# A two-layer CIN kernel: all chunk pairs of the second layer in Strassen's form, four equal stages, half of each T2 on VectorE

## The chip, the cores and the metric

The kernel runs on one core of a Trainium2 chip. The metric is device microseconds from launch to end; each time given is a median of several executions. The profile is one execution taken by the hardware profiler; its span runs from the first instruction to the last. In it PE is TensorE (PEld its weight loads), DVE is VectorE, ACT is ScalarE, POOL is GpSimd and SP the engine that issues most transfers.

## The reference, cut to what matters

```python
ROWS, FIELDS, EMB = 4096, 32, 16

def _cin_layer(out, x, W, b, gamma, beta):
    r, _, e = x.shape
    h = jnp.einsum('rne,rfe->rnfe', out, x).reshape(r, -1, e)    # all products of two fields
    h = jnp.einsum('rce,oc->roe', h, W) + b[None, :, None]       # 128 outputs
    return _batchnorm(h, gamma, beta)                            # mean and variance over rows and e

h1 = _cin_layer(x, x, W1, b1, g1, beta1)                         # 32*32 products
out, direct1 = (h1[:, :64], h1[:, 64:])
direct2 = _cin_layer(out, x, W2, b2, g2, beta2)                  # 64*32 products
return jnp.concatenate([direct1, direct2], axis=1).sum(axis=-1)
```

A site is one (row, e); there are 65,536. Each layer multiplies fields of a site with each other, contracts the products with a weight matrix to 128 outputs, and normalizes. All is fp32.

## The kernel before

The first layer (up to about 490 us of the span) works on 128 tiles of 512 sites and is not touched. The second layer works on `NC = 64` pairs of tiles; index `c` is the pair. The contraction over 2048 products is cut into 16 chunks of 128: four stages (`STAGES = (3, 0, 1, 2)`, index `k` in the order run, `i` the value), and in each stage two chunk pairs `q = 0, 1`. For one chunk pair the work is a product of 2 x 2 blocks: the weights give blocks a11, a21, a12, a22 (64 outputs of the 128, one of the two chunks), the field products give b11, b12, b21, b22 (one of the two tiles, one of the two chunks). The ordinary form needs 8 matmul calls of 128 x 64 weights against 128 x 512 products. Strassen's form (in Winograd's variant) needs seven, X1 to X7, with sums of weights (`s_sb`, made once) and sums of products:

- T3 = b22 - b12 comes out of the multiplication itself, since `bx` holds differences of inputs;
- T2 = b11 + T3, T1 = b22 - T2, T4 = b21 - T2 are made by vector engines.

In a stage, ScalarE makes two factors (`factor`, L646: the first layer's kept output, normalized, into PSUM), VectorE makes two groups of products of 128 x 2048 (`multiply`, L636): `z[:, 0::3]` (b11, b21) from the first and `z[:, 1:3]` (T3, b22) from the second. GpSimd then makes T (`sum_products`, L672): T2 in one instruction of 1024 columns, T1 and T4 in one of 2048. Stage 3 in `i` (`PLAIN`, the first run) has its q = 0 in the ordinary form and only q = 1 in Strassen's; there (`sum_half`, L681) VectorE makes its single T2, reading a copy of b11 that ScalarE has put into PSUM, and GpSimd makes T1 and T4 in 1024 columns. For c = 0 the last stage is wholly ordinary.

Each matmul writes the lower or upper 64 partitions of a PSUM bank, and the calls alternate between the halves, so that two run beside each other. `Sums` (L655) holds four banks of the six in the pool: x11 (X1 in two parts, one for each half), x62, x34, x57. The matmuls X5 and X4 of a stage (`x54`) are queued behind X3 and X2 of the next, except in the last stage, where they come at once.

When the four stages of a pair are done, `combine` (L734) adds the banks into the four output blocks: two ScalarE evictions and an add for X1 (`both`, L741), then `e[:, 0]` (L747), `u2` on ScalarE, `u3` (L754), a copy of half of `u3` on ScalarE, two more adds (L759, L760), squares for the variance on ScalarE, and a reduction over 16 on VectorE (L779). It is a generator: its steps are taken between the instructions of the next pair's stages, by calls of `step()` at fixed places. `idle` holds small VectorE tasks (statistics of the first layer, differences of inputs) of which one is taken in a pair.

The order on each engine is written out by hand: `queue(engine, ...)` (L226) ties each instruction behind the one queued before on that engine. The pools limit how far an engine runs ahead: three buffers of z, two of t, two of PSUM for factors and the copy of b11 together (`factors`), one of each tile of `combine`.

Every VectorE add of the second layer is recorded at L634, every ScalarE copy and factor at L631, every matmul at L670; they are told apart by tile names (`th`, `both`, `u`, `e`, `f`, `b`).

Of the kernel before, what the change touches and what calls it, by code (L numbers as in the profile page):

```python
# [56 lines left out]
PLAIN = 3  # L58
STAGES = (3, 0, 1, 2)

MINUS = ((PLAIN, 0), (2, 0), (2, 1))
# [7 lines left out]
def tile_cin(ctx: ExitStack, tc: tile.TileContext, xa, xb, xr, w1, w1m, w2, bn, out):  # L69
# [191 lines left out]
    with ExitStack() as one:  # L261
# [31 lines left out]
        neg_sb = const.tile([P, len(MINUS), 2, KEEP], FP, tag="neg", name="neg_sb")  # L293
# [3 lines left out]
        def combine_weights():  # L297

            w = w2_sb.rearrange("p (i j) o -> p i j o", j=4)
            a11, a21, a12, a22 = (w[:, :, j : j + 2, m] for j in (0, 2) for m in (low, high))  # L300
            s1, s2, s3, s4 = (s_sb[:, k] for k in range(4))
            minus = []
            for k, (i, q) in enumerate(MINUS):
                minus.append((neg_sb[:, k, 0], a21[:, i, q], a11[:, i, q], ALU.subtract))
                nc.vector.tensor_scalar(neg_sb[:, k, 1], a21[:, i, q], -1.0, None, ALU.mult)
# [236 lines left out]
    hpool = ctx.enter_context(tc.tile_pool(name="hpool", bufs=1))  # L542
# [58 lines left out]
    nc.vector.tensor_copy(b2_swapped[low], b2[high])  # L601
# [53 lines left out]
    class Sums:  # L655


        def __init__(self):

            banks = [psum.tile([P, T], FP, tag="ps", name=name) for name in ("x11", "x62", "x34", "x57")]  # L660
            x11, x62, x34, x57 = self.banks = banks
            self.of = {
                6: x62[low], 2: x62[high], 3: x34[low], 4: x34[high], 5: x57[low], 7: x57[high], 1: x11[low], 0: x11[high]
            }
            self.started = set()
# [6 lines left out]
    def sum_products(z):  # L672

        t = tpool.tile([P, 3, 2, T], FP, tag="t", name="t")
        queue("pool", lambda: nc.gpsimd.tensor_tensor(t[:, 0], z[:, 1], z[:, 0], ALU.add))  # L675

        twice = t[:, 0].unsqueeze(1).to_broadcast([P, 2, 2, T])
        queue("pool", lambda: nc.gpsimd.tensor_tensor(t[:, 1:3], z[:, 2:4], twice, ALU.subtract))  # L678
        return t

    def sum_half(z, b11):  # L681

        t = hpool.tile([P, 3, 1, T], FP, tag="th", name="th")
        add(t[:, 0, 0], z[:, 1, 1], b11)
        twice = t[:, 0].to_broadcast([P, 2, T])
        queue("pool", lambda: nc.gpsimd.tensor_tensor(t[:, 1:3, 0], z[:, 2:4, 1], twice, ALU.subtract))  # L686
        return t

    class Stage:


        def __init__(self, sums_, i, z, t, plain, last):

            self.matmul, self.last, self.i = sums_.matmul, last, i
            self.w = [weights(i, q) for q in range(2)]
            self.b11, self.t3, self.b22, self.b21 = ([z[:, k, q] for q in range(2)] for k in range(4))
            self.qs = tuple(q for q in range(2) if q not in plain)

            self.t2, self.t1, self.t4 = ({q: t[:, k, q - self.qs[0]] for q in self.qs} for k in range(3))

        def two(self, low_first, *halves):
            for x, w, b, stop in halves if low_first else halves[::-1]:
                self.matmul(x, w, b, stop and x in self.last)

        def ordinary(self, low_first, q):
            a11, a21, a12, a22, s1, s2, s3, s4 = self.w[q]
            minus_s3, minus_a21 = (neg_sb[:, MINUS.index((self.i, q)), k] for k in range(2))
            for x, u, y, v in ((3, s4, 2, a11), (5, s1, 4, a21)):
                self.two(low_first, (x, u, self.b22[q], False), (y, v, self.b11[q], False))
            for x, u, y, v in ((3, minus_s3, 2, a12), (5, minus_a21, 4, a22)):  # L710
                self.two(low_first, (x, u, self.t3[q], q == 1), (y, v, self.b21[q], q == 1))

        def x1(self, low_first):

            halves = [(x, self.w[q][0], self.b11[q], True) for x, q in zip((1, 0), self.qs)]
            if len(self.qs) == 1 and not low_first:
                halves[0] = (0, *halves[0][1:])
            self.two(low_first, *halves)

        def products(self, low_first, x, kx, bx, y, ky, by):  # L720
            for q in self.qs:
                stop = q == 1
                self.two(low_first, (x, self.w[q][kx], bx[q], stop), (y, self.w[q][ky], by[q], stop))

        def x32(self, low_first):
            self.products(low_first, 3, 7, self.b22, 2, 2, self.b21)

        def x67(self, low_first):
            self.products(low_first, 6, 5, self.t2, 7, 6, self.t3)

        def x54(self, low_first):
            self.products(low_first, 5, 4, self.t1, 4, 3, self.t4)

    def combine(c, sums_):  # L734

        x11, x62, x34, x57 = sums_.banks
        both = cpool.tile([P, T], FP, tag="both", name="both")
        act(both[low], x11[high])
        act(both[high], x11[low], bias=b2[low])
        yield  # L740
        add(both, both, x11)  # L741
        yield

        e = cpool.tile([P, 2, T], FP, tag="e", name="e")
        if idle:
            dve(idle.pop(0))
        add(e[:, 0], both, x62)  # L747
        yield
        u2 = cpool.tile([P, T], FP, tag="u2", name="u2")
        act(u2[low], e[low, 0], bias=b2[low])  # L750
        act(u2[high], e[low, 0], bias=b2_swapped[low])
# [25 lines left out]
        yield  # L777
        dve(
# [4 lines left out]
        if c < MOST:  # L783
            queue("act", lambda: add_square(c, 1, e))
# [10 lines left out]
    steps = iter(())  # L795

    def step(count=1):
        for _ in range(count):
            next(steps, None)

    for c in range(NC):
        raw, b, bx = loaded(c)
# [14 lines left out]
        f1 = factor(raw[STAGES[0]], STAGES[0], 0)  # L817
        for k, i in enumerate(STAGES):

            z = z2pool.tile([P, 4, 2, T], FP, tag="zz", name="zz")  # L820
            if c == k == 0:

                f2 = factor(raw[i], i, 1)
                for q in range(2):
                    multiply_part(z[:, 0::3], f1, b, q)
                    multiply_part(z[:, 1:3], f2, bx, q)
                b11 = factors.tile([P, T], FP, tag="f", name="b11")
                act(b11, z[:, 0, 1])
            else:
                multiply(z[:, 0::3], f1, b)  # L830

            if k > 0:
                step()
            if c > 0 or k > 0:
                f2 = factor(raw[i], i, 1)
                if k == 2:

                    step()
                if i == PLAIN:
                    b11 = factors.tile([P, T], FP, tag="f", name="b11")  # L840
                    act(b11, z[:, 0, 1])
                multiply(z[:, 1:3], f2, bx)

            plain = (0,) if i == PLAIN else (0, 1) if c == 0 and k == 3 else ()
            if i == PLAIN:
                t = sum_half(z, b11)
            elif not plain:
                t = sum_products(z)
            if k in (1, 2):

                step()
            if k < 3:
                f1 = factor(raw[STAGES[k + 1]], STAGES[k + 1], 0)
            if k < 3:

                step()
# [3 lines left out]
            low_first = c % 2 == 0  # L860
            rest = not low_first
            last = range(8) if k == 3 else ()
            if c == 0 and k > 1:
                last = ((0, 1, 6, 7), (2, 3, 4, 5))[k - 2]
            stage = Stage(sums_, i, z, t, plain, last)
            if i == PLAIN:
                stage.ordinary(low_first, 0)
            if len(plain) == 2:
                stage.ordinary(rest, 0)
            else:  # L870
                stage.x1(low_first if i == PLAIN else rest)
                stage.x32(rest)
            if k > 0:
                waiting.x54(rest)
            if len(plain) == 2:
                stage.ordinary(rest, 1)
            else:
                stage.x67(rest)
                if k == 3:
                    stage.x54(rest)  # L880
            waiting = stage
# [8 lines left out]
        steps = combine(c, sums_)  # L890

    assert not sums_left
    step(8)
# [27 lines left out]
    with tc.issue_after(lasts["dve"].ins):  # L921
        step()
# [58 lines left out]
```

## Time and profile before

| | |
|---|---|
| time, median of 3 | 2084.3 us (2084.09 to 2085.0) |
| span of the profiled execution | 2082.0 us |
| granted TensorE clock, mean | 0.997 |
| VectorE, products of 128 x 2048 in layer two | 510 instructions, 583.3 + 582.4 us |
| GpSimd, T1 and T4 of 2048 columns | 191 instructions, 871.4 us, 4562 ns each |
| GpSimd, T2 of 1024 columns | 191 instructions, 453.1 us, 2372 ns each |
| VectorE, T2 of one half (`th`) | 64 instructions, 44.1 us, 689 ns each |
| VectorE waiting for PE before products of layer two | 54.3 us in 119 waits |

The chain of waits follows the work back from the last instruction to what released each step. A row of the timeline gives start and duration in us, engine, line, operation, output and input names, shapes, and in brackets the idle time before it and what ended it. Durations of neighbours can overlap a little, so the cost of an instruction in a full queue is read from the starts.

### The profile page before, as it was taken

How to read it: one execution, taken by the hardware profiler on the slowest of the kernel's cores; microseconds unless marked ns; L12 is line 12 of the kernel's file. 1: busy time of each engine (PE TensorE's matmuls, PEld its weight loads, DVE VectorE, ACT ScalarE, POOL GpSimd, SP SyncE). 2: the span in 40 equal slices, each digit the busy share in tenths (PEclk: the TensorE clock that was granted, in tenths of full speed). 3: DMA queues.
4: the chain of work that ended last, by engine and by line, in shares of the span. 5: the costliest groups of instructions: out<-in, count | busy, mean ns of one | idle time of the engine just before them, and what ended most of it. 6: DMA issues, size and time to landing. Idle time of an engine off the chain costs nothing.

```text
span 2082.0 us, 23630 instructions
## 1 busy us (share of the span) xinstructions
PE 2061.8 (99%) x8634; PEld 927.9 (45%) x8634; DVE 1901.4 (91%) x1391; ACT 998.9 (48%) x1594; POOL 1471.8 (71%) x453
## 2 busy tenths in 40 slices
PE   9999999999999999999999999999999999999996
PEld 4444444443444444444444444444444444444443
DVE  8998888888999999999999999999999999999995
ACT  4555555554544444444444445454444454444443
POOL 0000000003999999999999999999999999999995
PEclk9999999999999999999999999999999999999998
DMA  9999999997776788776777777767677777776761
GB/s 384 385 339 346 334 357 357 354 337 195 172 170 162 178 194 191 191 176 167 167 184 176 184 176 176 175 165 172 162 172 185 174 177 174 169 172 162 172 142 41
DMA packets 112020, 440.65 MB, mean 212 GB/s; under 512 B 13088, under 2 KB 13088, under 8 KB 103456
## 3 DMA queue, kind: packets, MB, share of 16 engines
q1 hardware_dynamic: 105456, 418.43, 74.5%
q10 hardware_dynamic: 6448, 20.72, 2.6%
q8 instruction: 67, 1.10, 0.2%
q14 instruction: 49, 0.40, 0.1%
HBM read 417.07 MB, written 22.02 MB: 211 GB/s over the span
## 4 chain that ended last, share of the span: by engine, by line
PE 75%; DVE 1%; ACT 0%; DVEq 0%; issue 0%; ACTq 0%
PE x L670 75%; DVE zz L644 0%; DVE zz L639 0%; DVE e L634 0%; DVE d L911 0%; ACT u L631 0%; DVE d L779 0%; ACT f L631 0%; DVEq L977 0%; DVE u L634 0%; DVE groups_x L774 0%; DVE groups L774 0%; ACT sd L139 0%; DVE mv L136 0%; DVE ss L157 0%
## 5 line engine op out<-in xcount | busy, mean ns | idle before, releaser
L670 PE MATMUL x<-zz,s_sb 128*64 128x512 f32 x2048 | 951.3, 592 | 0.9 <-PE ps L427 0.7
L670 PE MATMUL x<-zz,w_sb 128*64 128x512 f32 x2312 | 889.5, 592 | 0.0
L678 POOL TENSOR_TENSOR t<-zz,t 128x2048 f32<-128x2048 f32 x191 | 871.4, 4562 | 15.0
L670 PE MATMUL x<-t,s_sb 128*64 128x512 f32 x1528 | 691.1, 593 | 0.0
L639 DVE TENSOR_TENSOR zz<-f,b 128x2048 f32<-128x2048 f32 x255 | 583.3, 2287 | 55.0 <-PE x L670 54.3
L639 DVE TENSOR_TENSOR zz<-f,bx 128x2048 f32<-128x2048 f32 x255 | 582.4, 2284 | 4.3 <-ACT f L631 4.3
L631 ACT ACTIVATE f<-a,keep 128x512 f32<-128x512 f32 x512 | 393.2, 776 | 283.3 <-DVE zz L639 281.1
L675 POOL TENSOR_TENSOR t<-zz 128x1024 f32<-128x1024 f32 x191 | 453.1, 2372 | 83.8 <-PE x L670 78.9
L686 POOL TENSOR_TENSOR th<-zz,th 128x1024 f32<-128x1024 f32 x64 | 152.0, 2375 | 487.5 <-DVE th L634 487.4
L398 PE MATMUL ps<-z,w_sb 128*128 128x512 f32 x992 | 434.2, 595 | 0.7 <-DVE z L366 0.6
L670 PEld LDWEIGHTS x<-zz,w_sb 128*64 128x64 f32 x2312 | 290.9, 137 | 251.1 <-issue 250.1
L670 PEld LDWEIGHTS x<-zz,s_sb 128*64 128x64 f32 x2048 | 278.0, 137 | 246.4 <-issue 238.9
L670 PE MATMUL x<-t,w_sb 128*64 128x512 f32 x764 | 360.7, 594 | 0.0
L366 DVE TENSOR_TENSOR z<-a,b 128x2048 f32<-128x2048 f32 (+1 forms) x129 | 293.3, 2275 | 55.2 <-PE ps L398 43.8
L398 PEld LDWEIGHTS ps<-z,w_sb 128*128 128x128 f32 x992 | 185.8, 190 | 247.1 <-issue 239.3
L670 PEld LDWEIGHTS x<-t,s_sb 128*64 128x64 f32 x1528 | 206.4, 137 | 185.7 <-issue 167.8
L330 ACT ACTIVATE e<-ps,bn_sb 128x512 f32<-128x512 f32 x124 | 85.4, 688 | 223.7 <-PE ps L398 212.6
L569 ACT ACTIVATE unread<-e,center 128x512 bf16<-128x512 f32 x124 | 89.7, 724 | 120.4 <-DVE e L634 118.6
L670 PEld LDWEIGHTS x<-t,w_sb 128*64 128x64 f32 x764 | 101.8, 137 | 91.3 <-issue 81.0
L631 ACT ACTIVATE u<-e,bn_sb 64x512 f32<-64x512 f32 x64 | 46.4, 725 | 189.3 <-DVE e L634 189.3
L670 PE MATMUL x<-th,s_sb 128*64 128x512 f32 x256 | 130.7, 592 | 0.0
L670 PE MATMUL x<-zz,neg_sb 128*64 128x512 f32 x264 | 124.1, 592 | 0.0
(104 smaller groups left out, 1187.2 us busy)
## 6 DMA issues: line engine op xcount, KB each, us to landing
a<-h SPq DMA_DIRECT2D x256, 512.0 KB, 8.3
a<-in_xa SPq DMA_DIRECT2D x128, 512.0 KB, 6.3
b<-in_xb SPq DMA_DIRECT2D x128, 512.0 KB, 7.3
b<-in_xb SPq DMA_DIRECT2D x64, 1024.0 KB, 7.1
bx<-in_xb SPq DMA_DIRECT2D x64, 512.0 KB, 8.3
bx<-x SPq DMA_DIRECT2D x64, 512.0 KB, 9.9
h<-kept ACTq DMA_DIRECT2D x64, 256.0 KB, 5.6
r<-in_xr SPq DMA_DIRECT2D x16, 512.0 KB, 7.8
```

The costliest lines, as they stand in the source:

```text
L330: nc.scalar.activation(e, ps, AF.Identity, bias=b1)
L366: return nc.vector.tensor_tensor(z[:, k], a.rearrange("p (a t) -> p a t", a=2)[:, k].unsqueeze(2).to_broadcast([P, n, 2, T]), b.rearrange( ...
L398: nc.tensor.matmul(pss[t], w1_sb[:, m, :], z[:, m // 2, m % 2, :], start=(t == m == 0), stop=(t > 0 and m == 3))
L569: return nc.scalar.activation(unread, e[:, s], AF.Square, bias=center[:, s], accum_out=squares[:, s, c : c + 1])
L631: return queue("act", lambda: nc.scalar.activation(to, source, AF.Identity, **scale_bias))
L639: dve(lambda: nc.vector.tensor_tensor(z, a, b.rearrange("p (k q) t -> p k q t", k=2), ALU.mult))
L670: queue("pe", lambda: nc.tensor.matmul(self.of[x], w, b, start=start, stop=stop))
L675: queue("pool", lambda: nc.gpsimd.tensor_tensor(t[:, 0], z[:, 1], z[:, 0], ALU.add))
L678: queue("pool", lambda: nc.gpsimd.tensor_tensor(t[:, 1:3], z[:, 2:4], twice, ALU.subtract))
L686: queue("pool", lambda: nc.gpsimd.tensor_tensor(t[:, 1:3, 0], z[:, 2:4, 1], twice, ALU.subtract))
```

## The change

All eight chunk pairs of a pair of tiles take Strassen's form, so that no stage has an ordinary half, and the four stages are alike. To keep GpSimd's load in bounds, VectorE makes the upper half (q = 1) of T2 in every stage, reading b11 from PSUM, as `sum_half` did in one; GpSimd makes the other half and then T1 and T4 in 2048 columns. X1 now takes one half bank. X2 is kept in two parts: q = 1 goes to the half bank that is free beside X1 (x21), q = 0 beside X6 (x62); the two parts are merged by the add that makes output block C22, for which ScalarE writes one of them into the upper half of x57. That saves one add in `combine`. The matmuls X5 and X4 of a stage are always queued at the head of the next one, also across pairs. The steps of `combine` are placed anew, the last of them (the reduction) one pair later; for c = 0 the first stage is the ordinary one.

```diff
-PLAIN = 3
-MINUS = ((PLAIN, 0), (2, 0), (2, 1))
...
-            banks = [psum.tile([P, T], FP, tag="ps", name=name) for name in ("x11", "x62", "x34", "x57")]
+            banks = [psum.tile([P, T], FP, tag="ps", name=name) for name in ("x21", "x62", "x34", "x57")]
...
-                6: x62[low], 2: x62[high], 3: x34[low], 4: x34[high], 5: x57[low], 7: x57[high], 1: x11[low], 0: x11[high]
+                0: x21[low], 1: x21[high], 6: x62[low], 2: x62[high], 3: x34[low], 4: x34[high], 5: x57[low], 7: x57[high]
...
+    def sum_products(z, b11):
+
+        t2 = tpool.tile([P, 2, T], FP, tag="t2", name="t2")
+        t14 = tpool.tile([P, 2, 2, T], FP, tag="t14", name="t14")
+        queue("pool", lambda: nc.gpsimd.tensor_tensor(t2[:, 0], z[:, 1, 0], z[:, 0, 0], ALU.add))
+        add(t2[:, 1], z[:, 1, 1], b11)
+        twice = t2.unsqueeze(1).to_broadcast([P, 2, 2, T])
+        queue("pool", lambda: nc.gpsimd.tensor_tensor(t14, z[:, 2:4], twice, ALU.subtract))
+        return t2, t14
...
+        def x2(self):
+            for q, x in ((1, 0), (0, 2)):
+                self.sums.matmul(x, self.w[q][2], self.b21[q], self.ends)
+
+        def x31(self):
+            for q in range(2):
+                self.one(3, 7, self.b22, q)
+                self.one(1, 0, self.b11, q)
...
     def combine(c, sums_):
...
-        act(both[low], x11[high])
-        act(both[high], x11[low], bias=b2[low])
+        act(both[low], x21[high])
+        act(both[high], x21[high], bias=b2_swapped[high])
+        e = cpool.tile([P, 2, T], FP, tag="e", name="e")
+        act(e[high, 0], x21[low])
         yield
-        add(both, both, x11)
-        yield
-        add(e[:, 0], both, x62)
+
+        add(both, both, x62)
         yield
...
-        u3_low = cpool.tile([KEEP, T], FP, tag="u3l", name="u3_low")
-        act(u3_low, u3[high])
+        act(e[low, 0], u3[high])
+        act(x57[high], both[high])
         yield
+
         add(e[:, 1], u3, x34)
-        add(e[low, 0], u3_low, x57[low])
+        add(e[:, 0], e[:, 0], x57)
         yield
...
+                multiply(z[:, 0::3], f1, b)
+                if k == 1:
+
+                    next(steps, None)
+                f2 = factor(raw[i], i, 1)
                 b11 = factors.tile([P, T], FP, tag="f", name="b11")
                 act(b11, z[:, 0, 1])
+                if k == 1:
+
+                    next(steps, None)
                 multiply(z[:, 1:3], f2, bx)
+                t = sum_products(z, b11)
+
+            if k == 0:
+                next(steps_before, None)
+            elif k < 3:
+                next(steps, None)
+            elif idle:
+                dve(idle.pop(0))
             if k < 3:
                 f1 = factor(raw[STAGES[k + 1]], STAGES[k + 1], 0)
+            elif c + 1 < NC:
+                following = loaded(c + 1)
+                f1 = factor(following[0][STAGES[0]], STAGES[0], 0)
+
+            next(steps, None)
...
+            if waiting:
+                waiting.x54()
+            if c == k == 0:
+                stage.ordinary()
             else:
+                stage.x2()
+                stage.x31()
+                stage.x67()
+            if c > 0 or k > 0:
+                waiting = stage
...
-        steps = combine(c, sums_)
+        steps, steps_before = combine(c, sums_), steps
```

More of the change, by code (lines that the diff above doesn't have):

```diff
@@ L292, in tile_cin @@
         s_sb = const.tile([P, 4, 4, 2, KEEP], FP, tag="s", name="s_sb")
-        neg_sb = const.tile([P, len(MINUS), 2, KEEP], FP, tag="neg", name="neg_sb")
+        neg_sb = const.tile([P, 2, 2, KEEP], FP, tag="neg", name="neg_sb")
         b1, g1, beta1, b2, g2, beta2 = (bn_sb[:, k : k + 1] for k in range(6))
@@ L302, in combine_weights @@
             minus = []
-            for k, (i, q) in enumerate(MINUS):
-                minus.append((neg_sb[:, k, 0], a21[:, i, q], a11[:, i, q], ALU.subtract))
-                nc.vector.tensor_scalar(neg_sb[:, k, 1], a21[:, i, q], -1.0, None, ALU.mult)
+            for q in range(2):
+                minus.append((neg_sb[:, q, 0], a21[:, STAGES[0], q], a11[:, STAGES[0], q], ALU.subtract))
+                nc.vector.tensor_scalar(neg_sb[:, q, 1], a21[:, STAGES[0], q], -1.0, None, ALU.mult)
             for to, x, y, op in (
@@ L541, in tile_cin @@
     tpool = ctx.enter_context(tc.tile_pool(name="tpool", bufs=2))
-    hpool = ctx.enter_context(tc.tile_pool(name="hpool", bufs=1))
     cpool = ctx.enter_context(tc.tile_pool(name="cpool", bufs=1))
@@ L600, in tile_cin @@
     b2_swapped = const.tile([P, 1], FP, tag="b2s", name="b2_swapped")
-    nc.vector.tensor_copy(b2_swapped[low], b2[high])
+    for x, y in ((low, high), (high, low)):
+        nc.vector.tensor_copy(b2_swapped[x], b2[y])
     direct_stats = const.tile([P, ENDING // 2, 6], FP, tag="dstats", name="direct_stats")
@@ L658, in __init__ @@
         def __init__(self):
-            banks = [psum.tile([P, T], FP, tag="ps", name=name) for name in ("x11", "x62", "x34", "x57")]
-            x11, x62, x34, x57 = self.banks = banks
+            banks = [psum.tile([P, T], FP, tag="ps", name=name) for name in ("x21", "x62", "x34", "x57")]
+            x21, x62, x34, x57 = self.banks = banks
             self.of = {
-                6: x62[low], 2: x62[high], 3: x34[low], 4: x34[high], 5: x57[low], 7: x57[high], 1: x11[low], 0: x11[high]
+                0: x21[low], 1: x21[high], 6: x62[low], 2: x62[high], 3: x34[low], 4: x34[high], 5: x57[low], 7: x57[high]
             }
@@ L670, in matmul @@
             queue("pe", lambda: nc.tensor.matmul(self.of[x], w, b, start=start, stop=stop))
[L672 to L687, printed above, removed]
+    def sum_products(z, b11):
[6 more added lines that the diff above has]
+        return t2, t14
@@ L689, in tile_cin, with __init__ @@
     class Stage:
-        def __init__(self, sums_, i, z, t, plain, last):
-            self.matmul, self.last, self.i = sums_.matmul, last, i
+        def __init__(self, sums_, i, z, t, ends):
+            self.sums, self.ends = sums_, ends
             self.w = [weights(i, q) for q in range(2)]
             self.b11, self.t3, self.b22, self.b21 = ([z[:, k, q] for q in range(2)] for k in range(4))
-            self.qs = tuple(q for q in range(2) if q not in plain)
-            self.t2, self.t1, self.t4 = ({q: t[:, k, q - self.qs[0]] for q in self.qs} for k in range(3))
@@ L701, in two @@
[L701 to L732, printed above, removed]
+            if t is not None:
+                t2, t14 = t
+                self.t2, self.t1, self.t4 = ([x[:, q] for q in range(2)] for x in (t2, t14[:, 0], t14[:, 1]))
+        def one(self, x, k, b, q):
+            self.sums.matmul(x, self.w[q][k], b[q], self.ends and q == 1)
+        def ordinary(self):
+            for q in range(2):
+                a11, a21, a12, a22, s1, s2, s3, s4 = self.w[q]
+                minus_s3, minus_a21 = (neg_sb[:, q, k] for k in range(2))
+                for x, u, y, v in ((3, s4, 2, a11), (5, s1, 4, a21)):
+                    self.sums.matmul(x, u, self.b22[q])
+                    self.sums.matmul(y, v, self.b11[q])
+                for x, u, y, v in ((3, minus_s3, 2, a12), (5, minus_a21, 4, a22)):
+                    self.sums.matmul(x, u, self.t3[q])
+                    self.sums.matmul(y, v, self.b21[q])
@@ new lines, in x2, with x67, x54 @@
+        def x2(self):
+            for q, x in ((1, 0), (0, 2)):
+                self.sums.matmul(x, self.w[q][2], self.b21[q], self.ends)
+        def x31(self):
+            for q in range(2):
+                self.one(3, 7, self.b22, q)
+                self.one(1, 0, self.b11, q)
+        def x67(self):
+            for q in range(2):
+                self.one(6, 5, self.t2, q)
+                self.one(7, 6, self.t3, q)
+        def x54(self):
+            for q in range(2):
+                self.one(5, 4, self.t1, q)
+                self.one(4, 3, self.t4, q)
@@ L734, in combine @@
     def combine(c, sums_):
-        x11, x62, x34, x57 = sums_.banks
+        x21, x62, x34, x57 = sums_.banks
         both = cpool.tile([P, T], FP, tag="both", name="both")
-        act(both[low], x11[high])
-        act(both[high], x11[low], bias=b2[low])
+        act(both[low], x21[high])
+        act(both[high], x21[high], bias=b2_swapped[high])
+        e = cpool.tile([P, 2, T], FP, tag="e", name="e")
+        act(e[high, 0], x21[low])
         yield
-        add(both, both, x11)
-        yield
@@ L744, in combine @@
-        e = cpool.tile([P, 2, T], FP, tag="e", name="e")
-        if idle:
-            dve(idle.pop(0))
-        add(e[:, 0], both, x62)
+        add(both, both, x62)
         yield
         u2 = cpool.tile([P, T], FP, tag="u2", name="u2")
-        act(u2[low], e[low, 0], bias=b2[low])
-        act(u2[high], e[low, 0], bias=b2_swapped[low])
+        act(u2[low], both[low], bias=b2[low])
+        act(u2[high], both[low], bias=b2_swapped[low])
         yield
@@ L777, in combine @@
         yield
+        if c < MOST:
+            queue("act", lambda: add_square(c, 1, e))
+        yield
         dve(
@@ L782, in combine @@
         )
-        if c < MOST:
-            queue("act", lambda: add_square(c, 1, e))
         if c % 16 == 15 or c == MOST - 1:
@@ L794, in tile_cin @@
     sums_left = late_evictions
[L795 to L799, printed above, removed]
+    steps, steps_before = iter(()), iter(())
+    waiting = None
+    following = loaded(0)
+    f1 = factor(following[0][STAGES[0]], STAGES[0], 0)
     for c in range(NC):
-        raw, b, bx = loaded(c)
+        raw, b, bx = following
         sums_ = Sums()
@@ L815, in tile_cin @@
                 queue("act", lambda: store_difference(g))
-        f1 = factor(raw[STAGES[0]], STAGES[0], 0)
         for k, i in enumerate(STAGES):
             z = z2pool.tile([P, 4, 2, T], FP, tag="zz", name="zz")
+            t = None
             if c == k == 0:
@@ L826, in tile_cin @@
                     multiply_part(z[:, 1:3], f2, bx, q)
+            else:
+                multiply(z[:, 0::3], f1, b)
+                if k == 1:
+                    next(steps, None)
+                f2 = factor(raw[i], i, 1)
                 b11 = factors.tile([P, T], FP, tag="f", name="b11")
                 act(b11, z[:, 0, 1])
[L829 to L841, printed above, removed]
-                multiply(z[:, 1:3], f2, bx)
@@ L844, in tile_cin @@
[L844 to L851, printed above, removed]
+                if k == 1:
+                    next(steps, None)
+                multiply(z[:, 1:3], f2, bx)
+                t = sum_products(z, b11)
[5 more added lines that the diff above has]
+                dve(idle.pop(0))
@@ L852, in tile_cin @@
             if k < 3:
                 f1 = factor(raw[STAGES[k + 1]], STAGES[k + 1], 0)
-            if k < 3:
-                step()
+            elif c + 1 < NC:
+                following = loaded(c + 1)
+                f1 = factor(following[0][STAGES[0]], STAGES[0], 0)
+            next(steps, None)
             for _ in range(min(len(sums_left), 4 if c == NC - 1 else 1)):
                 queue("act", sums_left.pop(0))
-            low_first = c % 2 == 0
-            rest = not low_first
@@ L862, in tile_cin @@
[L862 to L869, printed above, removed]
-            else:
[L871 to L881, printed above, removed]
+            stage = Stage(sums_, i, z, t, k == 3)
+            if waiting:
+                waiting.x54()
+            if c == k == 0:
+                stage.ordinary()
+            else:
+                stage.x2()
[3 more added lines that the diff above has]
+                waiting = stage
@@ L889, in tile_cin @@
                     write_direct()
-        steps = combine(c, sums_)
-    assert not sums_left
-    step(8)
+        steps, steps_before = combine(c, sums_), steps
+    waiting.x54()
+    assert not sums_left and not idle
+    next(steps_before)
+    for _ in range(8):
+        next(steps)
     ss2 = const.tile([P, 2], FP, tag="ss2", name="ss2")
@@ L921, in tile_cin @@
     with tc.issue_after(lasts["dve"].ins):
-        step()
+        next(steps)
     scale(dy, 1, ss2)
```

## Prediction

> **What bounds the kernel now.** I read the engine totals first, then the chain of waits, then the second layer stage by stage, because totals mix two layers with different limits.
>
> ```profile
> PE 2061.8 (99%) x8634; PEld 927.9 (45%) x8634; DVE 1901.4 (91%) x1391; ACT 998.9 (48%) x1594; POOL 1471.8 (71%) x453
> ...
> PE 75%; DVE 1%; ACT 0%; DVEq 0%; issue 0%; ACTq 0%
> ```
>
> TensorE is busy 99% and is the chain. The page warns that busy PE isn't PE at its peak, so I take its pace from starts. The table by stretch, deep in layer two (busy time and count for PE, PEld, VectorE, ScalarE, GpSimd, then clock and DMA):
>
> ```profile
> 1500.00:2000.00 500.00, 500.00 (x2328) 229.97 (x2326) 463.79 (x307) 236.81 (x375) 470.50 (x144) 1.00 0.72 171
> ```
>
> 2328 matmul records in 500 us; each `matmul` call of this fp32 kernel leaves two records, so a call costs 2 x 500/2328 = 0.430 us when low and high halves alternate. A pair of tiles ("pair" below) has 57 calls: 57 x 0.430 = **24.48 us per pair**. VectorE (464 of 500) and GpSimd (470) are close behind. So a small gain on TensorE is capped by what the others cost; the timeline of VectorE prices those:
>
> ```profile
> 1205.56 2.28 DVE L639 TENSOR_TENSOR zz<-f,b 128x2048 f32<-128x2048 f32 x1
> 1207.76 0.68 DVE L634 TENSOR_TENSOR u<-u,x 128x512 f32<-128x512 f32 x1
> 1208.36 2.28 DVE L639 TENSOR_TENSOR zz<-f,bx 128x2048 f32<-128x2048 f32 x1
> ...
> 1214.62 1.21 DVE L779 TENSOR_REDUCE d<-e 128x64 f32<-128x1024 f32 x1
> 1215.74 2.28 DVE L639 TENSOR_TENSOR zz<-f,bx 128x2048 f32<-128x2048 f32 x1
> ...
> 510.98 2.28 DVE L639 TENSOR_TENSOR zz<-f,bx 128x2048 f32<-128x2048 f32 x1
> 513.37 0.69 DVE L634 TENSOR_TENSOR th<-zz,b 128x512 f32<-128x512 f32 x1
> 514.18 2.29 DVE L639 TENSOR_TENSOR zz<-f,b 128x2048 f32<-128x2048 f32 x1
> ```
>
> Read the start column: independent instructions overlap a little, so a product costs 2.20 (1205.56 to 1207.76), an add 0.60, the reduction 1.12 to 1.13. The add into `th`, which needs what the product just before it wrote, starts 2.39 after it (63 of 63 times), not 2.20. And the product after `th` starts 0.80 later, not 0.60: it needs a factor from ScalarE:
>
> ```profile
> 513.30 0.79 ACT L631 ACTIVATE f<-a,keep 128x512 f32<-128x512 f32 x1 [1.60 <-DVE zz L639]
> ```
>
> That factor takes the PSUM buffer which the product starting at 510.98 releases at its end (513.26), so it ends at 514.09.
>
> **What the Trainium skill says.** "VectorE: DVE Perf Modes", on `tensor_tensor` in fp32, has one result per cycle and (N+151)/0.96 ns: 2291 ns at 2048; the trace has 2284 to 2287. Its section "The DRAIN you can't avoid" says the next operation waits until the pipe is empty; here independent ones start 0.08 us before the recorded end and only the dependent one waits past it, so I use the measured starts. "GPSIMD Engine Reference", section Specifications, warns of contention with VectorE instructions of two SBUF inputs; the trace does not show it: 2.284 us beside a busy GpSimd, 2.275 in layer one with GpSimd idle. "TensorEngine Tiling (Array Packing)", section Key Properties, says column tiles run independently; the 0.430 us per call against 0.59 for one record agrees.
>
> **The change part by part.**
>
> *TensorE.* The ordinary form of one chunk pair takes 8 calls, Strassen's 7. Every pair drops from 57 to 56; the first pair has 58 (stage 0 ordinary throughout). Before, 64 x 57 + 2 = 3650 calls; after, 64 x 56 + 2 = 3586. 64 x 0.430 = 27.5 us less, if TensorE stays the bound: 24.05 per pair. Low and high halves still alternate throughout, so no pairing is lost.
>
> *VectorE.* Each stage now has an add for half of T2 (three more per pair), and one combine add goes (five to four). In the order the new loop queues them, with the starts above:
> - stage 0: product 2.20, product 2.39, T2 add 0.60, reduction 1.13 = 6.32
> - stage 1: product 2.20, `both` add 0.60, product 2.39, T2 add 0.60, `u3` add 0.60 = 6.39
> - stage 2: product 2.20, product 2.39, T2 add 0.60, two `e` adds 1.20 = 6.39
> - stage 3: product 2.20, product 2.39, T2 add 0.80 (nothing between it and the next product, so the factor is waited for) = 5.39
>
> Sum **24.49 us per pair**. TensorE would need 24.05: VectorE becomes the bound, at the very pace TensorE has now (24.48). By the same prices the old VectorE needed about 22.7 per pair.
>
> *GpSimd.* Per stage one sum of 512 columns and one subtraction of 2048. The first size isn't in the trace; from 2.37 (1024) and 4.56 (2048) a line gives 1.28. The alternative bound is the 1024-column price, 2.37, which would be 28 us per pair; I take 1.28, because these two rows lie near proportion to size. With 0.08 for dependence (2.45 between dependent starts against 2.37) and 4.52: 4 x 5.88 = 23.5 per pair. It fits under 24.49, and the least gap between the products that feed it (5.39) is caught up in the next stage. Hidden.
>
> *ScalarE.* Three more `b11` copies (0.60), three evictions of x21 (about 1.9 in place of 1.28), one copy into x57 (about 0.63). Its 48% leaves room; what matters is the queue. Behind the x21 evictions in stage 1 stands the second factor: by my count it ends 1.1 us before VectorE wants it. Behind the two copies that wait for `u3` stands the second factor of stage 2: it comes ready 0.03 late. I keep 0.03 x 62 = 2 us. The x34 bank of the new pair waits for x21's eviction, with 0.4 us to spare, and x57 for the `both` add, 0.1; TensorE has 0.4 per pair in hand, so these cost nothing. DMA queues and bytes stay the same.
>
> *Absolute time, VectorE as bound.* The first full product starts at 495.59 as before (a factor releases it in both). Pair 0: three stages without combine, 3 x 5.39, and one idle task (+0.40, since it fills the 0.20 bubble): 512.2. Pair 1: no reduction yet, centre work 1.43 (526.67 to 528.10 in the trace), one idle task: 5.39 + 6.39 + 6.39 + 1.43 + 5.39 + 0.40 = 25.4, to 537.6. Pairs 2 to 62: 61 x 24.49 = 1493.9, plus 14 idle tasks at 0.40 and three small ones, about 1.2: 2038.3. Pair 63: 6.32 + 6.39 + 6.39 + 1.2 (two statistics) + 2.20: the last product starts at 2060.8, ends at 2063.1. GpSimd then needs 5.9 (to 2069.0) and TensorE its last four calls, 1.9: 2070.9.
>
> ```profile
> 2065.07 0.69 DVE L634 TENSOR_TENSOR u<-u,x 128x512 f32<-128x512 f32 x1 [1.52 <-ACT u L631]
> ```
>
> This add is where the tail starts today; it would start at 2071.0, 5.9 later. The tail itself grows by one copy, 0.6. 2084.3 + 5.9 + 0.6 + 2 (stage 2 factor) = 2092.8, **about 2092 us**. The equal paces would give no change; the loss comes from idle tasks no longer hidden and from GpSimd and the last products, which now follow VectorE's end.
>
> **Rivals.**
> 1. *TensorE stays the bound.* For it: 99% busy, and if the two dependence gaps (4 x 0.19 and 0.20) vanished, VectorE would need 23.5. Against: the 2.39 is there every time. 2084.3 - 27.5 + about 2.7 of start-up stall (GpSimd delivers its first T only at about 506) + 0.6 = 2060.
> 2. *VectorE binds but some gaps close*, for instance because work slips between T2 and the product: 0.2 per pair, 2079.
> 3. *More waits*: ScalarE's order delays factors or GpSimd slips beyond 24.49. 0.2 per pair gives 2104; a bound of 28 us per pair (512 columns at 2.37) is the far end, above 2300, which I hold at 1%.
>
> **How the numbers follow.** VectorE as bound, 2084 to 2100: 0.67. Rival 1: 0.15. Rival 2: 0.08. Rival 3: 0.10. Faster by over 0.2% (below 2080.1): all of rival 1, some of rival 2: 0.20. Within 0.2% (to 2088.5): the rest of it and the lower edge of the main case, 0.13. Slower: 0.67. The range 2076 to 2104 leaves out rival 1 and the upper part of rival 3.
>
> **What would show it.** Right: VectorE nearly without idle time after about 600 us, products' waits on PE gone, PE at about 98%, with waits on GpSimd `t14` or VectorE; pair to pair 24.5; T2 adds 2.39 after their product. Wrong: products still waiting for PE, and 24.05 from pair to pair (rival 1); or waits for `f` before the second product in stages 1 and 2 (rival 3). A GpSimd sum of 512 columns far from 1.28 us would upset the third estimate.

## The result, and the profile after

The changed kernel takes **2100.18 us** (median of 4, 2099.82 to 2100.61) against 2084.65 beside it: ratio 1.0075, 95% interval 1.0057 to 1.0092. It is 15.5 us slower; the forecast was 7.7 us slower (2092, range 2076 to 2104). The second layer is no longer TensorE's, as the totals, the chain of waits and the stretch from 1500 to 2000 us of the changed kernel show (columns as before: busy time and count for PE, PEld, VectorE, ScalarE, GpSimd, then clock, DMA share, GB/s):

```profile
PE 2061.8 (98%) x8506; PEld 749.9 (36%) x8506; DVE 1980.9 (94%) x1517; ACT 1194.2 (57%) x1913; POOL 1490.2 (71%) x517
...
DVE 54%; PE 25%; issue 15%; ACT 3%; POOL 1%; DVEq 1%; DMA 0%; POOLq 0%; SPq 0%
```

```profile
1500.00:2000.00 500.00, 497.85 (x2280) 162.08 (x2278) 487.26 (x345) 296.42 (x473) 473.94 (x163) 1.00 0.71 172
```

PE is busy for 2061.8 us in both kernels, though 128 matmul records are gone: this number says nothing of pace. The records do: 2280 in 500 us against 2328, so TensorE gets through fewer calls in the same time than before, though it has fewer to make. The chain has moved to VectorE (54%, where PE had 75%). Its timeline, from one second product of stage 1 to the same one of the next pair:

```profile
1489.53 2.28 DVE L639 TENSOR_TENSOR zz<-f,bx 128x2048 f32<-128x2048 f32 x1
...
1501.78 2.28 DVE L639 TENSOR_TENSOR zz<-f,bx 128x2048 f32<-128x2048 f32 x1
1504.20 0.69 DVE L634 TENSOR_TENSOR t<-zz,b 128x512 f32<-128x512 f32 x1
1504.91 2.29 DVE L639 TENSOR_TENSOR zz<-f,b 128x2048 f32<-128x2048 f32 x1
...
1514.06 2.28 DVE L639 TENSOR_TENSOR zz<-f,bx 128x2048 f32<-128x2048 f32 x1
```

1514.06 - 1489.53 = **24.53 us per pair** (forecast 24.49). None of VectorE's products of layer two waits for PE any more (before: 54.3 us in 119 waits). The T2 add (`t<-zz,b`) starts 2.42 after the product that it reads, where an independent instruction starts after 2.20. The chain of waits of the same kernel says what stands between:

```profile
1489.61 2.21 DVE zz L639
1491.83 0.03 issue
1491.85 0.05 DVEq L634
1491.90 0.04 issue
1491.95 0.06 DVE t L634
```

The product ends at about 1491.82, an instruction on VectorE's own queue (DVEq, at the line of the add) follows it, and only then does the add start.

### The profile page after: what moved, and what is told of

Its sections match the earlier page's. It is cut to its first block, busy times and chain, and to the rows that moved or that the text cites. A ratio compares the mean times of both kernels' runs of the same rounds, so it can differ in the third digit from the quotient of the medians.

```text
span 2098.5 us, 24403 instructions
## 1 busy us (share of the span) xinstructions
PE 2061.8 (98%) x8506; PEld 749.9 (36%) x8506; DVE 1980.9 (94%) x1517; ACT 1194.2 (57%) x1913; POOL 1490.2 (71%) x517
## 4 chain that ended last, share of the span: by engine, by line
DVE 54%; PE 25%; issue 15%; ACT 3%; POOL 1%; DVEq 1%; DMA 0%; POOLq 0%; SPq 0%
DVE zz L639 44%; PE ps L398 20%; DVE e L634 4%; PE x L670 2%; ACT f L631 2%; DVE u L634 2%; DVE both L634 2%; PE ps L359 2%; DVE t L634 1%; POOL t L679 1%; PE ps L427 1%; DVE d L773 1%; DVEq L634 1%; DMA b<-in_xb 0%; ACT unread L568 0%
## 5 line engine op out<-in xcount | busy, mean ns | idle before, releaser
L679 POOL TENSOR_TENSOR t<-zz,t 128x2048 f32<-128x2048 f32 x255 | 1165.5, 4571 | 20.0
L670 PE MATMUL x<-t,s_sb 128*64 128x512 f32 x2040 | 944.9, 595 | 16.6 <-POOL t L679 14.0
L676 POOL TENSOR_TENSOR t<-zz 128x512 f32<-128x512 f32 x255 | 326.7, 1281 | 564.1 <-DVE zz L639 522.8
L670 PE MATMUL x<-zz,w_sb 128*64 128x512 f32 x2056 | 710.7, 592 | 0.0
L670 PE MATMUL x<-t,w_sb 128*64 128x512 f32 x1020 | 486.0, 599 | 0.0
L670 PEld LDWEIGHTS x<-zz,w_sb 128*64 128x64 f32 x2056 | 219.7, 137 | 146.4 <-issue 118.9
L631 ACT ACTIVATE b<-zz 128x512 f32<-128x512 f32 x255 | 153.3, 601 | 154.9 <-DVE zz L639 146.4
L634 DVE TENSOR_TENSOR t<-zz,b 128x512 f32<-128x512 f32 x255 | 175.6, 689 | 35.0 <-DVE zz L639 1.0
L336 ACT ACTIVATE ed<-ps,bn_sb 64x512 f32<-64x512 f32 x124 | 84.6, 683 | 2.3
L114 DVE BATCH_NORM_STATS2 stats<-e 128x6 f32<-128x512 f32 x124 | 85.0, 686 | 0.0
## 6 DMA issues: line engine op xcount, KB each, us to landing
b<-in_xb SPq DMA_DIRECT2D x64, 1024.0 KB, 10.2
bx<-in_xb SPq DMA_DIRECT2D x64, 512.0 KB, 10.2
```

The costliest lines, as they stand in the source:

```text
L114: nc.vector.bn_stats(self.stats[:, self.at, :], h)
L336: done = nc.scalar.activation(ed[to, :], ps[KEEP:, :], AF.Identity, bias=b1[KEEP:])
L631: return queue("act", lambda: nc.scalar.activation(to, source, AF.Identity, **scale_bias))
L634: return dve(lambda: nc.vector.tensor_tensor(to, x, y, ALU.add))
L670: queue("pe", lambda: nc.tensor.matmul(self.of[x], w, b, start=start, stop=stop))
L676: queue("pool", lambda: nc.gpsimd.tensor_tensor(t2[:, 0], z[:, 1, 0], z[:, 0, 0], ALU.add))
```

## The experiments

All ten kernels follow. The time of the kernel before beside them was 2083.7 to 2084.1 us.

**1. The T2 half on ScalarE.** Is it VectorE's load that sets the pace?

```diff
-        add(t2[:, 1], z[:, 1, 1], b11)
+        act(t2[:, 1], z[:, 1, 1])
...
-                b11 = factors.tile([P, T], FP, tag="f", name="b11")
-                act(b11, z[:, 0, 1])
```

> The changed kernel, but the upper half of T2 is written by a ScalarE copy of T3 in place of the VectorE add, and the copy of b11 into PSUM is dropped with it (left out: b11 in that half, so the output isn't the reference's). ScalarE has as many copies as before, TensorE and GpSimd the same work; VectorE loses four adds and their gaps, about 3 us per pair of tiles. Theory (VectorE's queue sets the pace of the changed kernel, 24.53 us per pair): TensorE takes over at 56 calls x 0.430 = 24.05 per pair, time 2060 to 2068. Rival (TensorE and GpSimd themselves pace it, VectorE is only busy beside them): within 5 us of 2100. Second rival (GpSimd at 5.88 per stage delays T1 and T4): 2068 to 2090, with long waits of PE for GpSimd.

Measured: 2096.76 us, ratio 1.0062 (1.0046 to 1.0079). That is far from the 2060 to 2068 of the theory and looks like the rival's win, but the experiment had put a new wait where the old work was. ScalarE's timeline in it, then VectorE's next product:

```profile
1505.61 0.63 ACT L631 ACTIVATE t<-zz 128x512 f32<-128x512 f32 x1 [3.28 <-POOL t L679]
1506.14 0.77 ACT L631 ACTIVATE f<-a,keep 128x512 f32<-128x512 f32 x1
```

```profile
1507.00 2.29 DVE L639 TENSOR_TENSOR zz<-f,b 128x2048 f32<-128x2048 f32 x1 [0.38 <-POOL t L676]
```

The copy starts 0.12 after the second product ends (1505.49), and the next factor stands behind it: it ends at 1506.91, and the next product starts at 1507.00. The releasers named in brackets only happened to end at that moment. So each stage had about 1.5 us of waiting in place of 0.8 us of adding. The run tells nothing on the question; it was done again with the order mended.

**2. The factor ahead of the copy.** Against the kernel of the first experiment, cut to what matters:

```diff
-        act(t2[:, 1], z[:, 1, 1])
+        next_factor()               # the factor of the next stage, queued first
+        act(t2[:, 1], z[:, 1, 1])
```

> As the kernel whose upper half of T2 is a ScalarE copy of T3 (left out: b11 in that half), but ScalarE makes the next factor ahead of that copy; in the other order each first product waited about 1.5 us behind the second one for a factor that stood behind the copy. Theory (VectorE's adds set the changed kernel's pace): now VectorE really is relieved, about 21.3 us per pair, and TensorE paces at 56 calls: 2050 to 2058, as in the kernel with the T2 adds behind the combine instructions. Rival (GpSimd and ScalarE cannot feed TensorE at that pace): above 2075.

Measured: **2053.17 us**, ratio 0.9851 (0.9836 to 0.9865). The stretch from 1500 to 2000 us:

```profile
1500.00:2000.00 500.00, 500.00 (x2334) 167.53 (x2331) 445.28 (x272) 304.15 (x485) 483.99 (x168) 1.00 0.71 173
```

VectorE is down to 445 of 500, and TensorE is back at 2334 records. With VectorE relieved, the same TensorE and GpSimd work runs 47 us faster, at 24.03 per pair. This is TensorE's pace for 56 calls (24.05 by the forecast).

**3. Order alone: the T2 add behind the combine instruction.** Not one instruction more or less. Condensed:

```diff
-                t = sum_products(z, b11)
-            if k == 0: next(steps_before, None)
-            elif k < 3: next(steps, None)
-            elif idle: dve(idle.pop(0))
+                def between():
+                    if k == 0: next(steps_before, None)
+                    elif k < 3: next(steps, None)
+                    elif idle: dve(idle.pop(0))
+                t = sum_products(z, b11, between)    # calls between() just ahead of the T2 add
```

> The changed kernel with the order on VectorE altered, no instruction more or less: in stages 0, 1 and 2 the combine instruction of that place (the reduction, u3, the two e adds; in stage 3 an idle task if there is one) is queued between the second product and the T2 add, not behind the add. Theory (the T2 add waits 0.22 us for the end of the product that it reads, and anything independent fills that): three gaps of 0.22 go, VectorE needs 24.53 - 0.66 = 23.87 per pair, under TensorE's 24.05; with idle tasks and ScalarE's extra work 2062 to 2076. Rival (the gap is a fixed cost of the add, or the later T2 delays GpSimd by as much): 2095 to 2102.

Measured: **2054.35 us**, ratio 0.9859 (0.9844 to 0.9874), so 29 us under the kernel before and 46 under the changed one, and under the 2062 to 2076 of the theory. It is a kernel that beats both. Its VectorE timeline in stages 0 and 1:

```profile
1498.72 2.28 DVE L639 TENSOR_TENSOR zz<-f,bx 128x2048 f32<-128x2048 f32 x1
1500.92 1.21 DVE L774 TENSOR_REDUCE d<-e 128x64 f32<-128x1024 f32 x1
1502.05 0.68 DVE L634 TENSOR_TENSOR t<-zz,b 128x512 f32<-128x512 f32 x1
1502.64 2.29 DVE L639 TENSOR_TENSOR zz<-f,b 128x2048 f32<-128x2048 f32 x1
...
1507.64 0.68 DVE L634 TENSOR_TENSOR u<-u,x 128x512 f32<-128x512 f32 x1
1508.23 0.69 DVE L634 TENSOR_TENSOR t<-zz,b 128x512 f32<-128x512 f32 x1
```

The reduction follows the product after 2.20, and the add follows the reduction after 1.13 and `u3` after 0.59: no gap is left in either stage. VectorE's own period is then 23.84 (seen for many pairs in a row), under TensorE's; TensorE's chain is unbroken again:

```profile
PE 96%; DVE 1%; ACT 1%; DMA 0%; POOL 0%; issue 0%; POOLq 0%; SPq 0%; DVEq 0%
```

**4. The same in all four stages.** The second `e` add is moved to stage 3, so that one instruction stands ahead of each T2 add.

```diff
         add(e[:, 1], u3, x34)
-        add(e[:, 0], e[:, 0], x57)
         yield
+        ...
+        add(e[:, 0], e[:, 0], x57)       # taken in stage 3, ahead of its T2 add
+        yield
```

> As the kernel with the T2 adds behind the combine instructions, but with one of them in every stage: reduction in stage 0, u3 in 1, the first e add in 2, the second e add in 3 (with the squares and statistics moved after it). Theory: all four gaps of 0.22 and the 0.12 wait for the factor in stage 3 go: VectorE 23.5 per pair, 0.5 under TensorE's 24.05, so idle tasks are hidden too: 2060 to 2066. Rival (GpSimd at 23.5 plus late T2 is the next bound): 2066 to 2085, with PE waiting for GpSimd in every stage. Rival (fixed cost): 2095 or more.

Measured: 2054.52 us, ratio 0.9860 (0.9845 to 0.9875). It equals the third experiment: once TensorE binds, the fourth gap is worth nothing. The theory's 2060 to 2066 was again too high.

**5. One add more on VectorE.** The slope.

```diff
         add(u3, u2, x57)
+        add(cpool.tile([P, T], FP, tag="u3b", name="u3_again"), u2, x57)
```

> The changed kernel with one more VectorE add per pair: the u3 add (u2 from SBUF, x57 from PSUM) is made a second time into a tile that nobody reads. Theory (VectorE has no slack): 0.60 x 64 = 38 us more, 2136 to 2142. Rival (the 290 us that the separate merge cost came from VectorE being short in general): far more than 38. Rival (VectorE has slack): 2100 to 2110. Against the separate merge, whose add had both inputs in SBUF and took 4.64 us beside GpSimd, this one has one input in PSUM: it should take 0.6 to 0.7.

Measured: 2133.58 us, ratio 1.0237 (1.0220 to 1.0254): 33.4 us over the changed kernel, 0.52 per pair, a little under the 2136 to 2142 of the theory and far from both rivals. The added instruction took 0.68 and started 0.59 after `u3`; the period went from 24.53 to 25.11. About 2.5 us were absorbed in pairs 17, 33, 49, 53 and 57, whose extra waits shrank (17, 33 and 49: from 0.74 over the period to about 0.16).

**6. The calls given back to TensorE,** in the changed kernel and in that of the third experiment. In both, two calls of stage 1 are made a second time in every second pair, 64 in all:

```diff
                 stage.x31()
+                if k == 1 and c % 2:
+                    stage.one(3, 7, stage.b22, 0)
+                    stage.one(1, 0, stage.b11, 0)
```

> The changed kernel with two more matmul calls in stage 1 of every second pair (X3 and X1 of q = 0 are added a second time, so the output differs): 64 calls more, which makes 3650, the number of the kernel before. Theory (VectorE paces, TensorE has 0.48 us per pair in hand): 2099 to 2104. Rival (TensorE's calls are on the path): 64 x 0.43 = 27 us more, 2127.

> The kernel with the T2 adds behind the combine instructions, with the same 64 calls more as in the changed kernel with calls given back (output differs in the same way). Theory (with the gaps gone TensorE paces): now they cost 64 x 0.43 = 27 us: 2079 to 2083. Rival (VectorE at 496 of 500 us busy still paces): 2054 to 2062.

Measured: 2100.35 us in the changed kernel (ratio to before 1.0077, 1.0062 to 1.0092), so the calls cost nothing; 2080.60 us in the reordered one (0.9984, 0.9977 to 0.9990), so they cost 26 us, 0.41 each. It is the most direct test here of which engine binds where. The calls that the change saves were worth nothing until the gaps were gone.

**7. The parts of the change undone: the merge, and the division of T2.** First the two parts of X2 merged by an add of their own:

```diff
-        act(x57[high], both[high])
...
-        add(e[:, 0], e[:, 0], x57)
+        add(e[low, 0], e[low, 0], x57[low])
+        add(e[high, 0], e[high, 0], both[high])
```

> The changed kernel with one part undone: the two parts of X2 are merged by an add of their own on VectorE (64 partitions, 0.59 us by start to start), in place of the ScalarE copy into x57; so one more VectorE add per pair and one ScalarE copy less. Theory (VectorE has no slack): 0.59 x 64 = 38 us more, 2138 (2130 to 2142). Rival (TensorE or GpSimd paces it and VectorE has 0.4 us per pair to spare): 2100 to 2113.

Measured: 2390.26 us, ratio 1.1472 (1.1454 to 1.1489): 290 us over the changed kernel, where both theories allowed about 40 at most. The new add, on VectorE, and GpSimd's instruction at that time:

```profile
1500.69 4.64 DVE L634 TENSOR_TENSOR e<-e,both 64x512 f32<-64x512 f32 x1
1505.36 2.29 DVE L639 TENSOR_TENSOR zz<-f,b 128x2048 f32<-128x2048 f32 x1
```

```profile
1500.25 4.54 POOL L679 TENSOR_TENSOR t<-zz,t 128x2048 f32<-128x2048 f32 x1
```

The add has 512 columns and takes 4.64 us; it ends 0.54 after GpSimd's instruction does (1504.79), which is about what such an add costs elsewhere (0.59 from start to start). Both its inputs are in SBUF. All other VectorE instructions with two inputs in this layer have one in PSUM. The mean over 64 such adds is 4.507 us, so 288.4 us in all, nearly the whole loss. The granted TensorE clock was 0.973 in this run against 0.997 before; TensorE, busy for 436 of 500 us, does not pace it.

Then the whole T2 on GpSimd:

```diff
-        queue("pool", lambda: nc.gpsimd.tensor_tensor(t2[:, 0], z[:, 1, 0], z[:, 0, 0], ALU.add))
-        add(t2[:, 1], z[:, 1, 1], b11)
+        queue("pool", lambda: nc.gpsimd.tensor_tensor(t2, z[:, 1], z[:, 0], ALU.add))
...
-                b11 = factors.tile([P, T], FP, tag="f", name="b11")
-                act(b11, z[:, 0, 1])
```

> The changed kernel with the division of T2 undone: GpSimd makes both halves in one instruction of 1024 columns, VectorE none, ScalarE no copy of b11. GpSimd then needs 2.45 + 4.52 = 6.97 per stage, 27.9 us per pair, against 23.5. Theory (the division of T2 is what makes four equal stages possible): GpSimd paces, 63 x 27.9 + 21 after a start at about 500, and a tail of 20 us: 2275 to 2305. Rival (GpSimd's load is hidden): under 2100.

Measured: 2295.82 us, ratio 1.1016 (1.0997 to 1.1034). GpSimd is busy 494 of 500 us and paces. Without the division of T2, the four equal stages take 212 us more than the kernel before.

**8. The T2 add with both inputs in SBUF.** Is it the source that held the merge?

```diff
-        add(t2[:, 1], z[:, 1, 1], b11)          # b11 copied to PSUM by ScalarE
+        add(t2[:, 1], z[:, 1, 1], z[:, 0, 1])
...
-                b11 = factors.tile([P, T], FP, tag="f", name="b11")
-                act(b11, z[:, 0, 1])
```

> The changed kernel, but the T2 add on VectorE reads b11 from z in SBUF and ScalarE's copy of b11 into PSUM is dropped: both inputs of the add are in SBUF now. Theory A (an add with two SBUF inputs does not run while a GpSimd instruction does, as the 4.64 us of the separate merge suggest): each T2 add stands still until the GpSimd instruction beside it ends, 1.3 to 5 us in place of 0.69, and GpSimd then waits for it; a stage takes 7 us or so, time 2250 to 2400. Theory B (the source does not matter): 2085 to 2100, a bit less than the changed kernel because the next factor no longer waits for the second product.

Measured: 2183.18 us, ratio 1.0474 (1.0459 to 1.0490). It is slower by 83 us than the changed kernel, with four ScalarE copies fewer per pair. Theory B is out; theory A's 2250 was too much. The groups of this kernel (count, busy time, mean ns):

```profile
L634 DVE TENSOR_TENSOR t<-zz 128x512 f32<-128x512 f32 x255 | 265.5, 1041 | 33.1 <-POOL t L679 0.5 <-DVE zz L639 0.5 <-PE x L670 0.5
```

```profile
L676 POOL TENSOR_TENSOR t<-zz 128x512 f32<-128x512 f32 x255 | 449.8, 1764 | 525.9 <-DVE zz L639 525.2
```

The add has 1041 ns on average (689 from PSUM) and GpSimd's sum of 512 columns 1764 (1281). The mean of the adds mixes two kinds. One of each, and then GpSimd beside them:

```profile
1502.95 0.69 DVE L634 TENSOR_TENSOR t<-zz 128x512 f32<-128x512 f32 x1
...
1508.78 1.19 DVE L634 TENSOR_TENSOR t<-zz 128x512 f32<-128x512 f32 x1
```

```profile
1502.97 1.81 POOL L676 TENSOR_TENSOR t<-zz 128x512 f32<-128x512 f32 x1
1504.86 4.57 POOL L679 TENSOR_TENSOR t<-zz,t 128x2048 f32<-128x2048 f32 x1
1509.39 1.73 POOL L676 TENSOR_TENSOR t<-zz 128x512 f32<-128x512 f32 x1
```

The first add starts 0.02 before GpSimd's sum: it keeps its 0.69, and the sum takes 1.81 in place of 1.28. The second starts while the long subtraction runs (1504.86 to 1509.43) and ends 0.54 after it, just as the add of the merge did. Of the 255 adds, 124 start 0.19 us or more before the end of a running subtraction; they take 0.74 to 1.86 and end 0.54 to 0.57 after it. Two start behind a running sum and end 0.55 after that; the other 129 keep 0.69. So the instruction that starts first runs through, and the other one waits for its end. Theory A had the mechanism right. Its time was too long, because an add meets only the last 1.3 us of the subtraction or less, or none of it.

How the waits add up to 83 us is not separated. The adds are 0.352 us longer on average (90 us in all), but GpSimd's sums are 0.483 longer too (123 us), and each engine sets how long the other is held. VectorE's own work alone does not set the pace here: pairs with an idle task of 0.60 on VectorE are no longer than pairs without (25.99 in both), since their held adds are shorter by as much.

## Why the prediction was right, and where its sizes were off

**VectorE becomes the bound: right.** Experiment 2 (VectorE relieved: -47 us), 5 (VectorE loaded: +33), and 6 (TensorE loaded: 0) show it from three sides. The sum of 24.49 missed by 0.04: the T2 add starts 2.42 after its product, not 2.39, four times; against that the step from the T2 add to the next product in stage 3 came out at 0.72 instead of 0.80. That the two misses nearly cancel is luck.

**GpSimd is hidden: right.** 512 columns took 1.281 us (the line through two sizes said 1.28), and the subtraction starts 1.36 after the sum.

**The sum of absolute times: 7.4 us short.** By its own terms (predicted, measured):
- Pair 2 starts at 537.6 by the forecast, 536.54 in fact (-1.1): in pair 0 no T2 add stands ahead of the first full product, which starts at 494.48, not 495.59.
- Pairs 2 to 62: 1502.7 us (1493.9 + 6.8 + 2), measured 1509.5 (+6.8). The period brought 61 x 0.04 = 2.4. What came above 24.53 per pair was 13.2 against 6.8 for idle tasks: an idle task costs 0.49, not 0.40, because the wait that it fills was 0.12 and not 0.20, and some early pairs paid up to 0.84; and sums over d2 on ScalarE cost three pairs 0.74 each. These sums were left out of the forecast. The 2 us for the factor of stage 2 did not come (2.21 between the two products), and by chance that offsets most of the 2.4.
- Pair 63 up to its last product: 22.5, measured 24.5 (+2.0). Two waits of 0.81, for factors behind the last statistics on ScalarE.
- The tail from there: 10.2 to the last `u3`, measured 10.4; and 0.6 more for the two copies, as said.

Together -1.1 + 6.8 + 2.0 + 0.2 = 7.9, against 7.4 measured; the runs of the changed kernel differ by 0.8 among themselves. So the term that was mis-sized is small work off the main queues. The forecast followed ScalarE's queue only through a regular pair; but any ScalarE instruction that delays a factor is VectorE's time once VectorE binds. In the timelines of the changed kernel, ScalarE in pair 17 and VectorE's product that waits for it:

```profile
924.42 0.63 ACT L573 ACTIVATE unread<-d 128x512 bf16<-128x512 f32 x1
...
925.15 0.78 ACT L631 ACTIVATE f<-a,keep 128x512 f32<-128x512 f32 x1
```

```profile
925.97 2.29 DVE L639 TENSOR_TENSOR zz<-f,bx 128x2048 f32<-128x2048 f32 x1 [0.66 <-ACT f L631]
```

**Rival 1 (TensorE stays the bound)** fell for the reason given, and its time was nearly right for the kernel where its condition holds: it said 2060 if the dependence gaps vanished. They vanish by order alone in experiment 3, and the time is 2054.

**A reading that failed.** I wrote that the trace does not show the contention that the Trainium skill's "GPSIMD Engine Reference" (section Specifications) names for VectorE instructions with two SBUF inputs. The row I used could not show it: these products take their factor from PSUM, and in layer one, where both inputs are in SBUF, GpSimd is idle. Experiments 7 and 8 make the case: 4.507 and 1.041 us on average in place of 0.68 and 0.69. They agree with the page, and they show what two odd-looking pieces of the change buy: the merge through x57 (290 us) and the copy of b11 into PSUM (83 us).

**The gap.** "VectorE: DVE Perf Modes", section "The DRAIN you can't avoid", says that a read of what the previous VectorE operation wrote needs a semaphore or an operation in between, and, for a chain of copies, that a semaphore after each costs nothing extra. In this kernel a wait on the instruction just before is not free: the add starts 0.22 us later than an independent instruction would, and with one operation in between it starts without delay. No run separates the semaphore from the dependence, since every such add has both. The section also says that an operation which is not held starts earlier, which the prediction left out; the 2.20 between independent instructions agrees with it.

Left open: in pairs 53 and 57 one T2 add starts 2.77 after its product, 0.35 later than elsewhere, which is the 0.36 us that these pairs took over the period. In the chain of waits the instruction on VectorE's own queue is over at 1804.61 in pair 53, and for the next 0.40 us the add waits for nothing that the profile shows. What held it was not tried.

## What to carry to other kernels

Work saved on the engine that binds is worth only the distance to the next engine: add up every engine for one period, by starts and not by durations, before work is moved from one to another. An instruction that reads what the one before it on VectorE wrote costs a gap; put an independent one between, as here, where order alone turned +15.5 us into -29. When an experiment takes work off an engine, look whether it has put a wait in its place before it is believed.

## What the runs showed of the hardware

- A VectorE add with both inputs in SBUF does not run beside a GpSimd `tensor_tensor`; the one that starts first holds the other to its end. An add of 512 columns that started 0.44 us behind a GpSimd instruction of 4.54 took 4.64; adds that started just ahead of GpSimd's sum kept 0.69, and the sum took about 1.8 in place of 1.28. With one input in PSUM the add took 0.68 to 0.69 beside the same GpSimd work.
- A VectorE add that waits for the product just before it starts 0.22 us later (2.42 against 2.20); one instruction in between hides it.
- GpSimd `tensor_tensor` on fp32: 1.281 us for 512 columns, 2.37 for 1024, 4.56 to 4.57 for 2048.
